# Two GroupNorm attention layers on one core: v twice-split from the third job, job 1's statistics by VectorE, and weight preparation spread over four attentions

## The chip, the cores and the metric

The kernel runs on one core of a Trainium2 chip. TensorE multiplies matrices, VectorE (DVE in the profile) and ScalarE (ACT) work on tensors element by element, GpSimd (POOL) here only starts transfers that add into memory, and SyncE (SP) starts the other transfers. Each engine takes its instructions in a fixed order. The metric is the device time of one execution in microseconds: 3188.19 us is the median of three runs of the kernel before (3187.46 to 3192.82).

## The reference

The input x is 8 images of 512 channels and 32 by 32 points, in fp32. Two layers follow one another, of one form with weights of their own. Cut to what is computed for one image:

```python
xg = x.reshape(8, -1)                                   # 8 groups of 64 channels
xn = (xg - mean(xg)) * rsqrt(var(xg) + 1e-5) * gamma + beta
q, k, v = Wq @ xn + bq, Wk @ xn + bk, Wv @ xn + bv      # 512 x 512 on 512 x 1024
for head in range(8):                                   # d = 64, s and t are points
    a = softmax(q_h.T @ k_h * 64 ** -0.5, axis=-1)      # 1024 x 1024
    out_h = v_h @ a.T
x = x + Wp @ out + bp
```

## The kernel before

**Jobs and stages.** One image in one layer is a job. Sixteen jobs run in the order images 0 and 1 in layer 0, the same images in layer 1, then images 2 and 3 in layer 0, and so on. So jobs 0 and 1 are layer 0, jobs 2 and 3 layer 1. Stages alternate. The attention A(n) of job n computes scores, exponentials and values. The projection stage P(n+1) then computes v of job n+1, the output projection of job n, and k and q of job n+1. P0 stands ahead of all, and a last output projection of job 15 at the end.

**Projections.** Products of 512 by 512 weights with 512 by 1024 activations use the Strassen-Winograd scheme, which makes seven block products out of eight, with sums of blocks made before (factors of the weights, sums of the activations) and after (VectorE additions of the products). The scheme is applied once (`v_phase`, L552: seven products of half size, 56 matmuls) or twice (`deep_phases`, L645: 49 products of quarter size). K, Q and the output (O) are twice-split in every stage but the very last; v is once-split for the jobs below `DEEP_V` and twice-split from it on. The lists `ORDER`, `OUTER`, `OUTER_V` say in which order the seven outer products go.

**Weight factors.** A twice-split product needs 49 factors of each weight. They are made once and kept in device memory, and each outer product's seven come in as one tile of 448 KB. They are made in two ways. `deep_round` (L212) takes a whole raw weight in, makes the outer factors by four additions (512 elements on each partition), the inner ones by four more (896), and stores seven tiles. A `prepare` (L199) instead makes the inner factors of one outer block when that block comes in for its first use, in a projection stage, by four short additions, and stores them. A once-split weight, or one to be prepared, needs its outer factors first: `put_first` loads raw weights, makes four additions for each (`factor`, L159) and stores them (`store_factors`, L170). `ROUNDS` and `FIRST` (L55, L56) say in which attention which weight and layer is done. Rounds, raw weights, the sums for twice-split projections (`deep_steps`, L1337) and `w_last` of the very last projection all take one buffer, the tag "deep", one after the other.

**Fetches.** A ring of up to six weight tiles is fetched ahead by `fetch` (L178) along `plan`. These tiles, the exponentials of the attention and parts of projection results share a pool of twelve buffers, given out in turn: a tile waits until the last readers of the tile that held its buffer are done.

**Attention.** 64 steps, in eight groups of eight (a group is two heads and half of the queries). A step computes scores of 128 keys by 1024 (L1112), their exponentials on ScalarE (L1117), and the values (L1163). VectorE sums the exponentials of a group into `acc` for the denominators (L1131, L1133). Of a group's eight tiles the first four are added as two pairs: GpSimd starts a transfer that adds one tile into another (L1140), and VectorE adds the result (L1143). At a group's end `take` brings the values out of PSUM (L1184 on ScalarE, L1186 on VectorE) and `reduce` sums `acc` over partitions (L1198). After each second group the denominators are gathered by small transfers (`r<-r`, L1221), inverted (L1225 on), written to memory (`rd<-rt`, L1238), broadcast back (`rb<-rd`, L1240), and multiplied in (L1255). The last pair does this without transfers, at the `times` set under `ends`.

**What sets the order.** The orders of TensorE, ScalarE and VectorE are the program's. `put` places a chore at an attention step and moves on to the next step where one is there; `moves` holds transfers by step; `later` and `advance` place small steps by a planned clock of 1.71 us a step. The orders of SP and GpSimd are made by the tile framework from the program and its plan of times. Norm steps: eight `stat` reads (L283), a gather by transfers, `groups`, `factors` (L355), four `apply` passes on ScalarE (L360), then four sums of xn (`sums`, L1305). For job 1 the statistics are instead eight ScalarE passes, `Norm.sums` (L293) and `Norm.squares` (L301). For jobs 2 to 4 the reads lie in the projection stages P1 to P3; from job 5 on in the attention before.

Of the kernel before, what the change touches and what calls it, by code (L numbers as in the profile page):

```python
# [19 lines left out]
P = 128  # L20
# [19 lines left out]
NW = 7  # L40
# [13 lines left out]
DEEP_V = 4  # L54
ROUNDS = {0: (O, 0), 2: (O, 1), 3: (V, 0), 4: (V, 1)}  # L55
FIRST = {0: ((V, 1),), 1: ((K, 1), (Q, 1))}  # L56
# [25 lines left out]
def fast_path(  # L82
# [129 lines left out]
    def deep_round(which, layer):  # L212
# [17 lines left out]
        def store_outer():  # L230
            w = box[0][:, :, 0:4, :].rearrange("p f (c h) o -> p f c (h o)", c=2)
            store_factors(w, layer, which)

# [10 lines left out]
        return start, first, store_outer, second, [lambda o=o: store(o) for o in OUTER]  # L244
# [159 lines left out]
    def norm_steps(n):  # L404
# [5 lines left out]
        def factors():  # L410
            norm.factors(slice(0, NC))
            if n > 1:
                place()

        if n == 1:
            reads = [place] + [lambda cc=cc: norm.sums(cc) for cc in range(NC)]
            reads.append(norm.less_mean)
            reads += [lambda cc=cc: norm.squares(cc) for cc in range(NC)]
            reads.append(lambda: (norm.by_count(), norm.gather()))
            return reads, [norm.groups, factors] + [lambda cc=cc: norm.apply(cc) for cc in range(NC)]  # L420
# [587 lines left out]
    def last_weights(n):  # L1008
        w = acts.tile([P, NW, 2, CH], F32, tag="deep", name="w_last")
        layer = jobs[n][1]  # L1010
        load_blocks(w, layer, O)
        for s in (slice(S1, NW), slice(S3, S3 + 1)):
            nc.sync.dma_start(w[:, s], factors[O, layer][:, s])
        return w
# [76 lines left out]
    class Attention:  # L1091
# [101 lines left out]
        def reduce(self, g):  # L1193
# [65 lines left out]
            if ends:  # L1259
                times = (0.0, 0.2, 7.6, 8.2) if n + 1 >= DEEP_V else (0.0, 0.2, 2.0, 4.0)  # L1260
            for at, step in zip(times, (gather, invert, spread, normalise)):
                later(at, step)
# [288 lines left out]
    for n in range(-1, len(jobs)):  # L1551
        last = n + 1 == len(jobs)
        outs = None
        if n >= 0:
# [7 lines left out]

            def put_round(which, layer):
                load, first, store_outer, second, stores = deep_round(which, layer)
                moves[9] = load
                at = 12
                for fn in first:
                    at = put(at + 1, fn)
                if (which, layer) == (O, 1):
                    moves[at + 1] = store_outer  # L1570
                    at += 4
                for fn in second:
                    at = put(at + 1, fn)
                at = max(at, 30 if n == 0 else 25)
                for i, fn in enumerate(stores):
                    at += 1 + i % 2
                    moves[at] = fn

            def put_first(weights):
                at = 43 if n == 0 else 5  # L1580
                box = []

                def start():
                    box.append(acts.tile([P, 2, NW, 2, CH], F32, tag="deep", name=f"raw_{n}"))
                    for i, (which, layer) in enumerate(weights):
                        load_blocks(box[0][:, i], layer, which)

                moves[at] = start
                at += 3
                for i, (which, layer) in enumerate(weights):  # L1590
                    for part in range(4):
                        at = put(at + 1, lambda i=i, part=part: factor(box[0][:, i], part))
                    moves[at + 1] = lambda i=i, which=which, layer=layer: store_factors(
                        box[0][:, i], layer, which
                    )

            if last:
                w = last_weights(n)
                for i, fn in enumerate(last_sums(0)):
                    put(49 + 3 * i, fn)  # L1600
            else:
                for i, (_, fn) in enumerate(extra):
                    put(2 + i, fn)
                at = (10, 19, 22, 24, 26, 28, 36, 39, 42, 45)
                if n == 0:
                    for i, fn in zip((3, 3, 4, 5, 6, 8, 10, 11, 12, 13, 15), reads):
                        put(i, fn)
                    at = (22, 30, 34, 35, 37, 38, 41, 44, 47, 50)
                elif n >= DEEP_V:
# [3 lines left out]
                elif n + 1 == DEEP_V:  # L1613
                    at = (10, 19, 22, 24, 26, 28, 30, 32, 35, 38)
                for i, fn in zip(at, steps):
                    put(i, fn)
                if n in ROUNDS:
                    put_round(*ROUNDS[n])
                if n in FIRST:
                    put_first(FIRST[n])  # L1620
# [4 lines left out]
                if n + 1 >= DEEP_V:  # L1625
                    for at, fn in zip((37, 39, 41, 43, 45, 47, 49, 51), deep_first):
                        put(at, fn)
                else:
                    for at, fn in zip((57, 58, 59, 60), deep_first[4:]):
                        put(at, fn)  # L1630

                def begin_plan():
                    extend_plan(n + 1)
                    if n + 1 < DEEP_V:
                        for _ in range(RING):
                            fetch()

                put(61 if n + 1 < DEEP_V else 58, begin_plan)
                if n + 1 >= DEEP_V:
                    for at in (58, 59, 60, 61, 62, 63):  # L1640
                        moves[at] = fetch
            assert max([*chores, *moves], default=0) < NT * len(att.groups)
# [27 lines left out]
            if last:  # L1670
                for i, fn in enumerate(last_sums(1)):
                    later(7.0 + 0.8 * i, fn)
# [13 lines left out]
            if n == 1:  # L1686
# [269 lines left out]
```

## Time and profile before

| What | us |
|---|---|
| Median of three runs | 3188.19 |
| The profiled execution | 3193.6 |
| Its span in the profile | 3191.7 |
| Matmul busy time | 3160.1 |
| VectorE busy time | 2612.1 |
| ScalarE busy time | 2312.2 |
| GpSimd busy time | 283.6 |

The profile is of one execution, so that each duration in the text is one of that execution. Matmuls are pipelined and their ends are modelled. A wait is put down to the releaser that came last. An attention followed by a projection stage takes 195.7 us from job 5 on. The last attention lies from 3048.0 to 3158.2 us of the span, and the last projection's matmuls end at 3184.2.

### The profile page before, as it was taken

How to read it: one execution, taken by the hardware profiler on the slowest of the kernel's cores; microseconds unless marked ns; L12 is line 12 of the kernel's file. 1: busy time of each engine (PE TensorE's matmuls, PEld its weight loads, DVE VectorE, ACT ScalarE, POOL GpSimd, SP SyncE). 2: the span in 40 equal slices, each digit the busy share in tenths (PEclk: the TensorE clock that was granted, in tenths of full speed). 3: DMA queues.
4: the chain of work that ended last, by engine and by line, in shares of the span. 5: the costliest groups of instructions: out<-in, count | busy, mean ns of one | idle time of the engine just before them, and what ended most of it. 6: DMA issues, size and time to landing. Idle time of an engine off the chain costs nothing.

```text
span 3191.7 us, 61670 instructions
## 1 busy us (share of the span) xinstructions
PE 3160.1 (99%) x23925; PEld 1872.0 (59%) x23925; DVE 2612.1 (82%) x3541; ACT 2312.2 (72%) x4169; POOL 283.6 (9%) x318
## 2 busy tenths in 40 slices
PE   9989999999999999999999999999999999999998
PEld 7356383573845738466393664837548375573844
DVE  8797787868979788797888969789697887978957
ACT  6747666486777868777686776867768687686863
POOL 0100101001000010100101000010000100001000
PEclk9999999999999999999999999999999999999999
DMA  7645565465655455355564545446456463444743
GB/s 276 151 133 151 121 200 142 120 188 135 204 158 145 120 110 172 74 145 164 139 190 83 158 103 138 125 94 177 132 137 182 90 199 66 135 122 95 221 91 77
DMA packets 189162, 451.70 MB, mean 142 GB/s; under 512 B 38088, under 2 KB 56896, under 8 KB 188864
## 3 DMA queue, kind: packets, MB, share of 16 engines
q1 hardware_dynamic: 140016, 298.27, 27.4%
q0 software_dynamic: 48848, 149.44, 25.8%
q8 instruction: 190, 3.11, 0.4%
q14 instruction: 108, 0.88, 0.1%
HBM read 246.76 MB, written 50.26 MB: 93 GB/s over the span
## 4 chain that ended last, share of the span: by engine, by line
PE 81%; DVE 3%; DMA 1%; issue 1%; ACT 0%; SPq 0%; DVEq 0%; ACTq 0%
PE sc L1112 23%; PE po L1163 22%; PE zd L817 9%; PE vd L817 9%; PE yd L817 4%; PE ud L817 4%; PE vd L812 3%; PE zd L812 3%; PE ud L812 1%; PE yd L812 1%; DVE acc L1133 1%; PE z L564 0%; DVE acc L1143 0%; PE z_last L1055 0%; DMA r<-r 0%
## 5 line engine op out<-in xcount | busy, mean ns | idle before, releaser
L1117 ACT ACTIVATE e<-sc 128x1024 f32<-128x1024 f32 x1024 | 1043.8, 1025 | 575.8 <-PE sc L1112 539.5
L1163 PE MATMUL po<-e,v 64*64 64x512 f32 x8192 | 1060.1, 590 | 9.8 <-ACT e L1117 9.8
L1112 PE MATMUL sc<-q,k 64*64 64x512 f32 x8192 | 1058.5, 590 | 2.2 <-ACT e L1117 2.0
L1163 PEld LDWEIGHTS po<-e,v 64*64 64x64 f32 x8192 | 313.3, 133 | 576.9 <-issue 540.2
L1112 PEld LDWEIGHTS sc<-q,k 64*64 64x64 f32 x8192 | 310.7, 133 | 566.7 <-issue 506.9
L1133 DVE TENSOR_TENSOR acc<-acc,e 128x1024 f32<-128x1024 f32 x320 | 389.4, 1217 | 42.2 <-ACT e L1117 31.9
L1140 POOL DMA_DIRECT2D e<-e x224 | 192.4, 859 | 1766.2 <-ACT e L1117 1279.8
L1143 DVE TENSOR_TENSOR acc<-acc,e 128x1024 f32<-128x1024 f32 x224 | 272.4, 1216 | 10.9 <-DMA e<-e 9.1
L1131 DVE TENSOR_TENSOR acc<-e,e 128x1024 f32<-128x1024 f32 x128 | 156.4, 1222 | 146.9 <-ACT e L1117 146.9
L817 PE MATMUL zd<-deep,w 128*128 128x256 f32 x860 | 240.2, 379 | 0.0
L817 PE MATMUL vd<-deep,w 128*128 128x256 f32 x804 | 223.5, 379 | 0.0
L817 PEld LDWEIGHTS zd<-deep,w 128*128 128x128 f32 x860 | 163.2, 190 | 22.5 <-ACT ud L512 0.3
L817 PEld LDWEIGHTS vd<-deep,w 128*128 128x128 f32 x804 | 152.7, 190 | 20.8
L1198 DVE TRANSPOSE_TENSOR_REDUCE r<-acc 128x32 f32<-128x1024 f32 x128 | 159.3, 1245 | 4.3
L912 POOL DMA_DIRECT2D x<-p x61 | 72.9, 1195 | 969.8 <-ACT p L834 427.1
L859 DVE TENSOR_TENSOR p<-p,s 128x512 f32<-128x512 f32 x185 | 127.2, 688 | 30.0 <-ACT p L834 22.3
L859 DVE TENSOR_TENSOR q<-q,s 128x512 f32<-128x512 f32 x64 | 44.1, 689 | 84.5 <-ACT q L836 44.1
L817 PE MATMUL vd<-os,w 128*128 128x256 f32 x372 | 107.2, 379 | 0.0
L812 PE MATMUL vd<-w,deep 128*128 128x128 f32 x720 | 102.2, 275 | 1.1 <-ACT ud L512 1.1
L817 PE MATMUL zd<-os,w 128*128 128x256 f32 x348 | 97.3, 379 | 1.3 <-ACT yd L508 1.3
L1186 DVE TENSOR_TENSOR q<-po,px 128x512 f32<-128x512 f32 x116 | 79.0, 681 | 22.7 <-ACT px L1184 22.5
L859 DVE TENSOR_TENSOR k<-k,s 128x512 f32<-128x512 f32 x64 | 44.2, 691 | 64.1 <-ACT k L834 42.8
(294 smaller groups left out, 4875.1 us busy)
## 6 DMA issues: line engine op xcount, KB each, us to landing
w<-deep SPq DMA_DIRECT2D x385, 448.0 KB, 5.1
e<-e POOLq DMA_DIRECT2D x224, 512.0 KB, 4.7
x<-p POOLq DMA_DIRECT2D x61, 512.0 KB, 6.8
rb<-rd SPq DMA_DIRECT2D x96, 256.0 KB, 3.7
x<-x_dram SPq DMA_DIRECT2D x28, 512.0 KB, 6.9
out_dram<-x SPq DMA_DIRECT2D x28, 512.0 KB, 4.1
deep<-w SPq DMA_DIRECT2D x28, 448.0 KB, 3.9
deep<-round SPq DMA_DIRECT2D x28, 448.0 KB, 4.7
```

The costliest lines, as they stand in the source:

```text
L812: nc.tensor.matmul(ps[:, tokens], moving[i][:, tokens], lhs[:, FACTOR[i], :], start=(start and ti == 0), stop=True, skip_group_check=True,)
L817: nc.tensor.matmul(ps, lhs[:, FACTOR[i], :], moving[i], start=start, stop=True, skip_group_check=True,)
L859: nc.vector.tensor_add(to_, to_, five.to_broadcast([P, 2, QT]))
L1112: nc.tensor.matmul(sc[h * HD : (h + 1) * HD, j, :], k[r, hp, k0 : k0 + HD], q[r, hp, sh * HALF : (sh + 1) * HALF], start=True, stop=True,)
L1117: nc.scalar.activation(e, sc, AF.Exp, scale=SCALE)
L1131: nc.vector.tensor_add(acc[g], self.es[i - 1], e)
L1133: nc.vector.tensor_add(acc[g], acc[g], e)
L1140: nc.gpsimd.dma_start(self.summed[i], self.summed.pop(i - 1), accum_op=ALU.add)
L1143: nc.vector.tensor_add(self.acc[g], self.acc[g], self.summed.pop(i))
L1163: nc.tensor.matmul(po[g][j * HD : (j + 1) * HD, h, :], v[r, kc, d0 : d0 + HD], e[r, j, :], start=(kc == 0), stop=(kc == NT - 1),)
L1186: nc.vector.tensor_add(to_, p[:, 1, :], px)
L1198: nc.vector.tensor_reduce(self.r[:, 0, m, :], self.acc.pop(g).rearrange("p j (b e) -> p (j b) e", e=RP), AX.X, ALU.add, apply_transpose=True,)
```

## The change

The change has six parts.

1. `DEEP_V` goes from 4 to 2: v of jobs 2 and 3 is twice-split. The conditions on `DEEP_V` move with it: from A1 on the attention is followed by the combined stage with v's sums made in the attention (`deep_steps`, all eight), and the last pair's `times` are the longer ones.
2. Rounds: O of layer 0 stays in A0, V of layer 1 moves from A4 to A1, O of layer 1 stays in A2, V of layer 0 stays in A3. The outer factors of layer 1's V are no longer made. K's of layer 1 are made in A0 and Q's in A1, where both were made in A1.
3. Job 1's statistics are made in A0 by `stat` on VectorE, at the steps at which the later attentions have theirs, and no longer by ScalarE. The reads for jobs 3 and 4 move from P2 and P3 into the attentions that follow these, A2 and A3; only those for job 2 stay in P1.
4. Placing: norm steps, round, deep sums and raw loads get other steps; the six fetches go one a step from 59 in every attention; transfers get a `move` that seeks the next free step, as `put` does.
5. The outer factors of layer 1's O are not stored. The last attention makes them from the raw blocks by four additions at steps 12, 14, 16 and 18. The last normalisation is at 7.0 on the planned clock (8.2 before), its transpose at 2.0 (7.6 before), and the last sums begin at 7.1 (7.0 before).
6. The second layer's output bias is made in P1 in place of P2.

```diff
-DEEP_V = 4
-ROUNDS = {0: (O, 0), 2: (O, 1), 3: (V, 0), 4: (V, 1)}
-FIRST = {0: ((V, 1),), 1: ((K, 1), (Q, 1))}
+DEEP_V = 2
+ROUNDS = {0: (O, 0), 1: (V, 1), 2: (O, 1), 3: (V, 0)}
+FIRST = {0: (K, 1), 1: (Q, 1)}
...
-        if n == 1:
-            reads = [place] + [lambda cc=cc: norm.sums(cc) for cc in range(NC)]
-            reads.append(norm.less_mean)
-            reads += [lambda cc=cc: norm.squares(cc) for cc in range(NC)]
-            reads.append(lambda: (norm.by_count(), norm.gather()))
-            return reads, [norm.groups, factors] + [lambda cc=cc: norm.apply(cc) for cc in range(NC)]
         reads = [lambda cc=cc, sh=sh: norm.stat(cc, sh) for cc in range(NC) for sh in range(2)]
...
         load_blocks(w, layer, O)
-        for s in (slice(S1, NW), slice(S3, S3 + 1)):
-            nc.sync.dma_start(w[:, s], factors[O, layer][:, s])
         return w
...
                 times = (0.0, 0.2, 7.6, 8.2) if n + 1 >= DEEP_V else (0.0, 0.2, 2.0, 4.0)
+                if n + 1 == len(jobs):
+                    times = (0.0, 0.2, 2.0, 7.0)
...
             def put_round(which, layer):
-                load, first, store_outer, second, stores = deep_round(which, layer)
-                moves[9] = load
-                at = 12
+                load, first, second, stores = deep_round(which, layer)
+                begin = {0: 6, 1: 12}.get(n, 9)
+                move(begin, load)
+                at = begin + 3
                 for fn in first:
                     at = put(at + 1, fn)
-                if (which, layer) == (O, 1):
-                    moves[at + 1] = store_outer
-                    at += 4
                 for fn in second:
                     at = put(at + 1, fn)
-                at = max(at, 30 if n == 0 else 25)
+                at = max(at + 3, 25)
                 for i, fn in enumerate(stores):
-                    at += 1 + i % 2
-                    moves[at] = fn
-
-            def put_first(weights):
-                at = 43 if n == 0 else 5
+                    at = move(at + 1 + i % 2, fn)
+
+            def put_first(which, layer):
+                at = move(37 if n == 0 else 3, lambda: start()) + 3
...
             if last:
                 w = last_weights(n)
+                for part in range(4):
+                    put(12 + 2 * part, lambda part=part: factor(w, part))
...
-                at = (10, 19, 22, 24, 26, 28, 36, 39, 42, 45)
-                if n == 0:
-                    for i, fn in zip((3, 3, 4, 5, 6, 8, 10, 11, 12, 13, 15), reads):
-                        put(i, fn)
-                    at = (22, 30, 34, 35, 37, 38, 41, 44, 47, 50)
-                elif n >= DEEP_V:
+                if n == 1:
+                    at = (8, 14, 15, 16, 18, 19, 21, 24, 27, 30)
+                else:
                     for i, fn in zip((3, 3, 4, 5, 5, 6, 7, 7, 8), reads):
                         put(i, fn)
                     at = (16, 22, 23, 24, 26, 27, 29, 31, 33, 35)
-                elif n + 1 == DEEP_V:
-                    at = (10, 19, 22, 24, 26, 28, 30, 32, 35, 38)
+                    if n < DEEP_V + 2:
+                        at = (17, 23, 24, 25, 27, 28, 30, 32, 34, 36)
...
                 if n + 1 >= DEEP_V:
-                    for at, fn in zip((37, 39, 41, 43, 45, 47, 49, 51), deep_first):
+                    for i, fn in enumerate(deep_first):
+                        put((42 if n in ROUNDS else 37) + 2 * i, fn)
+                else:
+                    for at, fn in zip((50, 52, 54, 56), deep_first[4:]):
                         put(at, fn)
-                else:
-                    for at, fn in zip((57, 58, 59, 60), deep_first[4:]):
-                        put(at, fn)
-
-                def begin_plan():
-                    extend_plan(n + 1)
-                    if n + 1 < DEEP_V:
-                        for _ in range(RING):
-                            fetch()
-
-                put(61 if n + 1 < DEEP_V else 58, begin_plan)
-                if n + 1 >= DEEP_V:
-                    for at in (58, 59, 60, 61, 62, 63):
-                        moves[at] = fetch
+                move(58, lambda: extend_plan(n + 1))
+                for _ in range(RING):
+                    move(58, fetch)
...
-            if n == 1:
+            if n == 0:
                 load, bias_steps = make_out_bias(1)
```

## The prediction

> **What bounds the kernel.** The busy shares first: TensorE is busy 99% of the span and the chain that ended last lies on it for 81%, so other engines matter only where TensorE waits for them.
>
> ```profile
> PE 3160.1 (99%) x23925; PEld 1872.0 (59%) x23925; DVE 2612.1 (82%) x3541; ACT 2312.2 (72%) x4169; POOL 283.6 (9%) x318
> PE 81%; DVE 3%; DMA 1%; issue 1%; ACT 0%; SPq 0%; DVEq 0%; ACTq 0%
> ```
>
> Then the stages, cut at the first matmul of each. Columns: start and end, length, busy time of PE, PEld, DVE, ACT, POOL, granted clock, DMA share, GB/s. The rows are A0, P1, A1, P2, A2, P3, A3, P4, A4, P5, A5 (A an attention, P a projection stage).
>
> ```profile
> 78.80:196.90 118.10, 111.69 (x1026) 39.15 (x1025) 90.82 (x115) 80.67 (x92) 12.93 (x15) 0.97 0.59 145
> 196.90:286.80 89.90, 88.05 (x410) 76.90 (x406) 72.26 (x109) 62.73 (x156) 4.79 (x4) 1.00 0.46 135
> 286.80:396.90 110.10, 110.10 (x1026) 39.32 (x1025) 86.50 (x104) 73.17 (x76) 13.23 (x15) 1.00 0.57 136
> 396.90:487.00 90.10, 88.31 (x411) 76.64 (x407) 79.49 (x161) 59.98 (x156) 4.77 (x4) 1.00 0.62 189
> 487.00:604.30 117.30, 111.81 (x1026) 38.55 (x1025) 91.73 (x115) 72.91 (x76) 17.26 (x15) 0.99 0.58 137
> 604.30:697.80 93.50, 90.88 (x410) 78.63 (x406) 69.92 (x104) 62.74 (x156) 5.99 (x5) 0.97 0.60 180
> 697.80:807.90 110.10, 110.10 (x1025) 39.06 (x1024) 93.30 (x113) 73.18 (x76) 12.61 (x15) 1.00 0.56 133
> 807.90:895.80 87.90, 86.25 (x491) 77.83 (x490) 71.54 (x102) 74.48 (x196) 4.77 (x4) 1.00 0.65 206
> 895.80:1006.60 110.80, 110.61 (x1026) 38.67 (x1025) 100.59 (x123) 73.14 (x76) 12.59 (x15) 1.00 0.59 149
> 1006.60:1092.10 85.50, 85.50 (x494) 77.61 (x490) 67.62 (x99) 75.45 (x196) 4.77 (x4) 1.00 0.47 140
> 1092.10:1202.20 110.10, 110.10 (x1026) 39.07 (x1025) 95.23 (x115) 73.05 (x76) 12.62 (x15) 1.00 0.50 115
> ```
>
> The last two rows are the steady pair, 110.1 + 85.5 (85.6 between first matmuls), and TensorE never pauses in it. A0 and A2 lose 8.1 and 7.3 us, A4 0.7; P1 to P4 are 4.3, 4.5, 7.9 and 2.3 longer than steady. Beyond A4 nothing can be gained. The waits that end in A0:
>
> ```profile
> ACT e L1117 <- DVE acc L1143: 8.5, 1, 8.5
> DVE lt L1225 <- DMA r<-r: 7.0, 1, 7.0
> PE po L1163 <- ACT e L1117: 6.4, 1, 6.4
> ```
>
> Read upwards from TensorE: it waited 6.4 us for one exponential, which waited 8.5 us for a VectorE addition. Step 61 fetches six weight tiles at once from the twelve buffers that exponentials share, so the next exponential needs the buffer of a recent pair, and VectorE was late, after 7.0 us behind a gather. A2 has the same wait (3.4), and P1 and P3 open with 1.9 us behind `DVE q L1186`: VectorE's last addition is done 6.57 and 6.33 us after A0 and A3, against 1.24 after A5.
>
> **What the Trainium skill says.** "Perfetto Trace Analysis", Optimization Strategy: kernels have several regimes, and within one the gaps of the contended engine are followed to what they wait for. The table agrees: 99% hides 28 us in nine stages. "TensorE: Matmul & The Clock Gate", Part 1: an idle window of about 3.4 us halves the clock until TensorE has been busy again. A0 agrees: a 6.4 us wait, 8.1 lost, clock 0.97. "DMA: Bandwidth & Descriptors", Issuing engines are not separate DMA queues: all issuers share sixteen engines. The trace agrees: accumulating pair DMAs of A0 land after 5.1 us in the middle, but after 8.4 and 11.2 beside seven stores of 448 KB. "VectorE: DVE Perf Modes", The TRN2 errata: an fp32 addition takes (N+151)/0.96 ns; 1224 for 1024, measured 1217.
>
> **1. v twice-split for jobs 2 and 3.** Once-split v is 56 matmuls of 0.43 us, 24 us; twice-split it is 49 products of two 128-wide halves, 0.446 a product, 21.9. P2 and P3 lose 2.1 each. Their VectorE work grows by the deep v's additions, 13.3 for 2.7; in P2 the eight reads of statistics (6.3) and the output bias (2.9) leave, but the preparations of K and Q stay (each four factors of 0.29 and a wait for the tile): 79.5 + 10.6 − 9.2 = 81 of VectorE where a steady stage has 67, so I add 0.7. P2 85.6 + 0.7 = **86.3**, P3 and P4 **85.6**: the stalls at their openings go, because a deep v needs its second PSUM half later. P4 also loses 2.3: its attention no longer ends late.
>
> **2. Fetches one a step instead of six at once (A0), last deep sums at 50 to 56.** The exponential before the end then needs an addition about six steps old. Both TensorE waits of A0 and A2 (6.4 and 3.4, with the slow clock 8.1 and about 5) go if VectorE is no more than some 6 us behind. The cover is that slack.
>
> **3. Job 1's statistics.** Eight ACT passes leave A0, 4.2 + 4.6 + 1.6 for reading accumulators = 10.4 us of ACT (80.7 to 70). In come eight statistics on VectorE and four aggregations, 8×0.68 + 4×0.21, = 6.3 at steps 3 to 8. The factors of V1 (4×0.68) give way to K1's, the same. VectorE in A0: 90.8, and 5.3 that fell past its end (6.57 late for 1.24), and 6.3: 102 of 110. Not a bound, but little slack. P1 takes the bias (four steps, 2.9), so it keeps its late opening: **91** for 90.0 (1.9 of stall become about 3).
>
> **4. The queue of SP in A0.** Here the order changes. In the kernel before the broadcast of the first normalisation is issued ahead of the seven stores of the round; the next raw load (same single buffer) comes after them:
>
> ```profile
> 121.40 0.33 SPq L1238 DMA_DIRECT2D rd<-rt  x1
> 121.78 1.14 SPq L345 DMA_DIRECT2D mr<-dg  x2
> 123.01 1.26 SPq L1240 DMA_DIRECT2D rb<-rd  x2
> 124.37 7.13 SPq L239 DMA_DIRECT2D deep<-round  x7
> 141.68 2.76 SPq L157 DMA_DIRECT2D raw<-wqkv_dram  x4
> ```
>
> The round now starts at step 6 and the load of K1 stands ahead of `rd<-rt` on SP. From first store to load were 17.3 us; seven stores (3.1 MB) now begin about 38 us into A0, the load issues near 51, `rd` 52, `rb` 54, and 256 KB land about **60** (56 to 64). VectorE, in order, reaches that normalisation at 48, so it idles some 12 us; behind it stand the accumulations that free exponentials' buffers. 102 + 12 is 4 past the end, and with the usual 1.2 to 4 behind the last exponential the last addition falls some 8 us after A0. That is about the slack of part 2: TensorE is stalled, one to one, only if `rb` lands later than 61. With 0.9 for an exponential behind a late application (part 5): A0 = **111.0**, bounds 110.1 and 116.
>
> **5. Rounds V1 in A1 and V0 in A3, O1 in A2, none in A4; norm steps moved.** A round costs VectorE 7.1. A1: 86.5 + 7.1 − 2.7 (K1's factors) + 4.5 (a deep v's first sums) + some 3 fallen past its end = 98. A2 and A3 now have what A4 had, 100.6, and A4 lost 0.7; A4 now has A5's 95. A4's loss is this wait:
>
> ```profile
> 936.62 1.24 ACT L360 ACTIVATE xn<-x,off,mul 128x1024 f32<-128x1024 f32 x1 [0.79 <-DVE off L355]
> ```
>
> It made the exponential behind it 1.9 late; in A5 1.1 is free. In A2 and A3 the factors stand at step 23 (22 in A4), and in VectorE's order the inversion (1.7) now precedes them: 2.85 late − 1.15 free = 1.7. A2 and A3 **111.8** each, bounds 110.1 and 113.5; A1 **110.2**, A4 **110.1**.
>
> **6. The last output's factors** are made by four additions of 0.68 at steps 12 to 18 of the last attention (VectorE 78 busy of 110), in place of two loads and of a store in A2: nothing, under that slack; uncovered 2.7. Its final transpose comes 5.6 us sooner (7.6 to 2.0), the normalisation 1.2 sooner; the last stage's wait is on a residual addition queued after it, so nothing, at best −0.5.
>
> **Sum.** A0+P1 202.0 for 208.2: −6.2. A1+P2 196.5 for 200.3: −3.8. A2+P3 197.4 for 211.0: −13.6. A3+P4 197.4 for 198.0: −0.6. A4 −0.7. Total **−24.9** on the profiled execution, 3193.6 (span 3191.7) to 3168.7. The median of the runs is 5.4 lower; I take the same difference from it: **3163**. If those 5.4 were stalls that the change removes, it would be 3169.
>
> **Rivals.**
> (a) Nothing stalls: A0 110.1, P1 90, P2 85.6, A2 and A3 110.1. Saves 31.5: **3157**. For it: steady stages never pause. Against: the queue of part 4.
> (b) VectorE stays the late engine: `rb` lands at 64 to 68 (another 3 to 5 in A0, with the slow clock), or A1 to A3 and P2, at 98 to 101 and 81, pass 2 to 4 us on. +6 to +8: **3170**. For it: A4 before lost time at this load. Against: fetches need no recent buffer.
> (c) The change doesn't do what it says: only the matmuls saved show (4.1) and the waits return at other steps: **3184**, no change by the 0.2% (6.4 us) that this kernel's measurement can tell.
> (d) Slower: the queue of part 4. Each us that `rb` lands past 61 costs TensorE one. At 86 it has eaten the 25 us, and beyond about 92 the kernel is slower than before by over 0.2%: **3195** or more. Stores of 3.1 MB would have to take over 40 us, where 17.3 were seen.
>
> **Chances.** Forecast 0.48, (a) 0.17, (b) 0.25, (c) 0.05, (d) 0.05. Range 3155 to 3175: from (a) less 2 to (b) plus 5. Faster 0.91 (forecast, a, b, a little off (c)), same 0.05, slower 0.04.
>
> **What would show it.** `DVE q L1242` waiting about 12 us on `rb<-rd` in A0 (part 4; if under 4, part 4 is wrong). A0 near 111, P1 91, P2 to P4 85.5 to 86.5; applications waiting on `off` in A2 and A3 (part 5; if these are 110.1, it was too dark). No `po` wait over 1 us at the ends of A0 and A2 (part 2). If P2 stays above 88, VectorE's preparations bound it; if a stage after A4 differs by over 0.3, an edit counted at nothing was not.

## The result, and the profile after

The changed kernel takes 3184.99 us (median of 20 runs, 3181.07 to 3187.94) where the kernel before takes 3189.54 (20 runs, 3184.10 to 3192.84): a ratio of 0.9986, with a 95% interval from 0.9979 to 0.9993. It is faster by 4.5 us, not by the 25 that were forecast, and lies outside the range of 3155 to 3175. Its profiled execution took 3187.94 us (span 3186.2), 5.7 less than that of before; it is the slowest of the 20.

The shares of busy time of the changed kernel, and its chain of work that ended last, hardly differ:

```profile
PE 3156.2 (99%) x24093; PEld 1872.4 (59%) x24093; DVE 2637.2 (83%) x3571; ACT 2333.5 (73%) x4233; POOL 281.0 (9%) x318
PE 81%; DVE 1%; issue 0%; DMA 0%; ACT 0%; SPq 0%; POOL 0%; DVEq 0%; ACTq 0%; POOLq 0%
```

The table by stage, with the columns of the prediction, for A0, P1, A1, P2, A2, P3, A3, P4, A4 of the changed kernel:

```profile
80.20:199.20 119.00, 112.04 (x1026) 37.78 (x1025) 93.44 (x123) 73.43 (x77) 13.84 (x15) 0.99 0.58 135
199.20:293.40 94.20, 91.44 (x407) 79.21 (x408) 77.56 (x121) 62.56 (x156) 4.79 (x4) 0.96 0.52 153
293.40:403.40 110.00, 110.00 (x1025) 39.02 (x1024) 93.80 (x112) 73.12 (x76) 12.59 (x15) 1.00 0.62 157
403.40:491.40 88.00, 86.05 (x494) 77.76 (x490) 81.54 (x157) 74.22 (x196) 4.77 (x4) 1.00 0.64 193
491.40:605.50 114.10, 110.52 (x1025) 38.86 (x1024) 101.13 (x123) 73.12 (x76) 13.45 (x15) 1.00 0.58 143
605.50:691.10 85.60, 85.60 (x498) 77.66 (x494) 67.61 (x99) 75.46 (x196) 5.99 (x5) 1.00 0.66 197
691.10:806.10 115.00, 111.81 (x1025) 37.72 (x1024) 99.80 (x122) 73.36 (x76) 13.46 (x15) 0.99 0.59 143
806.10:891.70 85.60, 85.60 (x498) 77.65 (x494) 68.72 (x100) 75.43 (x196) 4.77 (x4) 1.00 0.62 190
891.70:1001.70 110.00, 110.00 (x1026) 39.00 (x1025) 92.83 (x113) 73.10 (x76) 12.59 (x15) 1.00 0.48 105
```

| Stage (us between first matmuls) | before | forecast | after |
|---|---|---|---|
| A0 | 118.1 | 111.0 | 119.0 |
| P1 | 89.9 | 91 | 94.2 |
| A1 | 110.0 | 110.2 | 110.0 |
| P2 | 90.1 | 86.3 | 88.0 |
| A2 | 117.3 | 111.8 | 114.1 |
| P3 | 93.5 | 85.6 | 85.5 |
| A3 | 110.2 | 111.8 | 115.1 |
| P4 | 87.9 | 85.6 | 85.5 |
| A4 | 110.8 | 110.1 | 110.0 |

A steady attention takes 110.03 us and a steady projection stage 85.54, together 195.6. P3, P4 and A4 are steady as forecast, and so are all later stages and the end. Five stages are not: A0 is 8.0 over the forecast, P1 3.2, P2 1.7, A2 2.3, A3 3.3, together 18.5. P0, counted from its first matmul of `z` (L553), is 71.3 for 70.1, 1.2 over; with it and the few tenths that A1 and others are under, the 19.2 between the forecast of 3168.7 and the profiled execution is accounted for. In kernels made from the changed one P0 lies between 69.9 and 72.3, in the profile of before and those of two kernels made from it between 69.9 and 70.3; what makes some 1 us of that is left open.

The waits of A0, those of TensorE, VectorE and ScalarE:

```profile
PE sc L1099 <- ACT e L1104: 3.4, 1, 3.4
PE po L1150 <- ACT e L1104: 3.4, 1, 3.4
DVE q L1242 <- DMA rb<-rd: 17.6, 2, 14.7
DVE lt L1212 <- DMA r<-r: 3.1, 1, 3.1
ACT e L1104 <- DVE acc L1118: 5.4, 2, 4.6
ACT xn L356 <- DVE off L351: 4.4, 1, 4.4
```

TensorE stands twice for an exponential: once in the middle, when ScalarE waits 4.4 us for the norm's factors, and once at the end, when that exponential has waited 4.6 us for an addition of VectorE, which is late after 14.7 us behind a broadcast. A2 and A3 have the first kind only. In A2's order of time, VectorE then ScalarE:

```profile
533.74 0.59 DVE L1212 TENSOR_REDUCE lt<-r 32x64 f32<-32x256 f32 x1 [1.75 <-DMA r<-r]
...
536.91 0.16 DVE L351 TENSOR_TENSOR off<-vec_sb,off 128x4 f32<-128x4 f32 x1
537.11 1.24 ACT L356 ACTIVATE xn<-x,off,mul 128x1024 f32<-128x1024 f32 x1 [4.00 <-DVE off L351]
```

The factors stand behind the inversion in VectorE's order, and the inversion waits for its gather. SP's order of time in A0:

```profile
118.58 7.85 SPq L235 DMA_DIRECT2D deep<-round  x7
131.17 0.38 SPq L157 DMA_DIRECT2D raw<-wqkv_dram  x1
131.61 0.46 SPq L1225 DMA_DIRECT2D rd<-rt  x1
132.11 1.45 SPq L157 DMA_DIRECT2D raw<-wqkv_dram  x3
134.16 2.26 SPq L1227 DMA_DIRECT2D rb<-rd  x2
```

It is the order that the prediction named: the first store, the raw load, `rd` and `rb` are issued 38.4, 51.0, 51.4 and 54.0 us after A0's start. The landing of `rb` is read from the end of VectorE's wait, at 66.5.

### The profile page after: what moved, and what is told of

It reads as the page before. It is cut to its first block, busy times and chain, and to the rows that moved or that the text cites. A ratio compares the mean times of both kernels' runs of the same rounds, so it can differ in the third digit from the quotient of the medians.

```text
span 3186.2 us, 62139 instructions
## 1 busy us (share of the span) xinstructions
PE 3156.2 (99%) x24093; PEld 1872.4 (59%) x24093; DVE 2637.2 (83%) x3571; ACT 2333.5 (73%) x4233; POOL 281.0 (9%) x318
## 4 chain that ended last, share of the span: by engine, by line
PE 81%; DVE 1%; issue 0%; DMA 0%; ACT 0%; SPq 0%; POOL 0%; DVEq 0%; ACTq 0%; POOLq 0%
PE sc L1099 23%; PE po L1150 23%; PE zd L806 9%; PE vd L806 9%; PE yd L806 4%; PE ud L806 4%; PE vd L801 4%; PE zd L801 3%; PE yd L801 1%; PE ud L801 1%; DVE acc L1120 0%; PE z_last L1042 0%; DMA r<-r 0%; ACT e L1104 0%; DVE x L1064 0%
## 5 line engine op out<-in xcount | busy, mean ns | idle before, releaser
L801 PE MATMUL vd<-w,deep 128*128 128x128 f32 x840 | 119.1, 275 | 1.1 <-ACT ud L501 1.1
L801 PE MATMUL zd<-w,deep 128*128 128x128 f32 x728 | 106.5, 275 | 0.9 <-ACT ud L501 0.9
L801 PEld LDWEIGHTS vd<-w,deep 128*128 128x128 f32 x840 | 106.2, 192 | 1.3 <-ACT ud L501 1.3
```

What stands on the lines that cost most here:

```text
L801: nc.tensor.matmul(ps[:, tokens], moving[i][:, tokens], lhs[:, FACTOR[i], :], start=(start and ti == 0), stop=True, skip_group_check=True,)
```

## The experiments

The theory at first: A0's first stall and those of A2 and A3 come from the place of the norm's factors (part 5 of the prediction), A0's second stall and P1's from SP's queue (part 4). The rival: VectorE has too much to do in these attentions, so that its waits only move. Kernels with one execution are read by their stages. A stage in which TensorE never waits repeats closely: A1 is 110.03 or 110.04 us in all 16 profiles. A stage with waits need not: A0 is 119.0 us in the changed kernel and 116.5 in a kernel whose one edit lies in A1, and P1 is 88.8 and 89.9 in two executions of one kernel. So in such stages a difference of up to some 2.5 us shows little by itself, and the waits are read with it.

**Factors at step 22 in A0, A2 and A3.**

```diff
-                    if n < DEEP_V + 2:
-                        at = (17, 23, 24, 25, 27, 28, 30, 32, 34, 36)
```

> The changed kernel, but the norm steps of A0, A2 and A3 take the steps of the later attentions (factors at 22, not 23), which puts the factors on VectorE ahead of the inversion, and of its wait for the gather. Theory (ScalarE's application waits 4.0 to 4.4 us for off, because off stands behind an inversion that waits for a gather): the wait falls to about 1, A2 goes from 114.1 and A3 from 115.1 to 110.0 to 110.8 each, A0 from 119.0 to 114.5; 12 us in all. Rival (VectorE is the bound in A2 and A3 with 101 us): they stay above 112, or P3 and P4 open with 2 us of waits instead of 85.5.

The rows of this kernel for A0, P1, A2 and A3:

```profile
81.50:195.60 114.10, 110.94 (x1025) 38.58 (x1025) 93.77 (x123) 73.40 (x77) 12.93 (x15) 1.00 0.59 142
195.60:289.50 93.90, 91.38 (x409) 79.26 (x409) 77.26 (x121) 62.26 (x156) 4.79 (x4) 0.96 0.52 152
486.80:597.60 110.80, 110.61 (x1026) 38.61 (x1025) 101.12 (x123) 73.14 (x76) 12.61 (x15) 1.00 0.59 147
683.10:793.90 110.80, 110.61 (x1026) 38.69 (x1025) 99.50 (x122) 73.14 (x76) 12.61 (x15) 1.00 0.60 146
```

A2 and A3 are 110.8 with VectorE as busy as before (101.1 and 99.5), and their P3 and P4 stay at 85.5: VectorE is no bound there. ScalarE's wait for `off` falls from 4.4 us to 0.5 in A0 and from 4.0 to 0.8 in A2. A0 is 4.8 shorter than the changed kernel's. The three together are 12.5 us, in a time of 3175.45: one step in the order of VectorE. P1 keeps 93.9, and VectorE still waits 14.3 us for the broadcast.

**The round of A0 at step 12, alone.**

```diff
-                begin = {0: 6, 1: 12}.get(n, 9)
+                begin = {0: 12, 1: 12}.get(n, 9)
```

> The changed kernel, but the round of A0 begins at step 12 instead of 6, so that SP issues the broadcast of the first normalisation ahead of the seven stores and of K1's raw load. Theory (the broadcast behind the raw load costs A0 its second stall of 3.4 us and some 1 us of slow clock, and P1 its 2.8 us wait and slow clock): the 14.7 us wait of VectorE on rb<-rd falls under 3, A0 goes from 119.0 to 114 to 115 (its first stall, behind the late off, stays), P1 from 94.2 to 90 to 91; 8 us in all. Rival (VectorE has too much work in A0, 102 us and more, so that its waits only move): A0 stays at 117 to 119 and P1 above 93.

A0 118.5, P1 94.6: nothing gained, as the rival said. VectorE's waits in A0:

```profile
DVE lt L1212 <- DMA r<-r: 9.5, 2, 7.8
...
DVE q L1242 <- DMA rb<-rd: 3.3, 1, 3.3
```

The broadcast is early now, but the second gather stands behind the same raw load, which waits for later stores. SP's order of time:

```profile
151.53 3.42 SPq L157 DMA_DIRECT2D raw<-wqkv_dram  x4
155.00 1.84 SPq L1208 DMA_DIRECT2D r<-r  x3
```

This run alone can't tell a moved queue from too much work.

**Without K1 in A0** (with factors at step 22).

```diff
                 if n == 0:
-                    put_first(*FIRST[n])
+                    factors[K, 1] = factors[Q, 0]
```

> The kernel with factors at step 22, and without the raw load, the four additions (2.7 us of VectorE) and the store of K1 in A0; layer 1's K takes its outer factors from another weight's store instead, so that part of the computation is left out. The broadcast follows the seven stores at once. Theory (what is left in A0, 4.1 us, and P1's 6 us over a quiet stage come from transfers of the attention queued behind the raw load, which waits for the stores): rb<-rd lands near 53 us after A0's start, VectorE waits under 6 for it instead of 14.3, A0 is 110 to 111, P1 90 to 91.5. Rival (VectorE's work after the middle of A0 is more than the time left, and its waits only move, as when the round was begun later): A0 stays at 113 or more and P1 above 93.

A0 is 111.2 and P1 91.7; VectorE waits 9.1 us for the broadcast, not under 6. Most of A0's loss is gone with the raw load, though the 2.7 us of additions left out may count too.

**K1's raw load by GpSimd** (with factors at step 22; the round at step 6, then at step 12).

```diff
-                nc.sync.dma_start(w[:, 2 * j + i], raw_block(layer, which, i, j))
+                queue.dma_start(w[:, 2 * j + i], raw_block(layer, which, i, j))
...
-                    load_blocks(box[0], layer, which)
+                    load_blocks(box[0], layer, which, nc.sync if n else nc.gpsimd)
```

> The kernel with factors at step 22 and K1's raw load issued by GpSimd instead of SP, the round of A0 at step 6 as in the changed kernel. It is the same computation as the changed kernel. Theory: the broadcast follows the stores directly and VectorE's 14.3 us wait falls to 5 to 7; A0 110 to 111.5, P1 90 to 91.5, A2 and A3 110.8, P2 87.3; in all 20 us below the changed kernel, some 3165. Rival: GpSimd, waiting for the stores with the raw load, holds up the pairs behind it and VectorE waits for e<-e instead; A0 stays at 113 or more, and the whole near 3172.

3168.86 us, a ratio to before of 0.9935 (0.9918 to 0.9952). A0 111.3, P1 92.0, VectorE's wait 8.6: A0 as expected, the wait longer than 5 to 7, and P1 and the time above what was expected.

> The kernel with factors at step 22, the round of A0 begun at step 12, and K1's raw load issued by GpSimd instead of SP, so that neither the first broadcast nor the second gather stands behind it. Theory: the waits of VectorE on r<-r and rb<-rd in A0, 7.8 and 3.3 when only the round was begun later, fall to under 5 together; A0 110 to 111.5, P1 90 to 92. Rival (the work itself): A0 above 113, P1 above 93.

A0 110.4, P1 88.8, a time of 3164.07. All work of A0 is there, additions too, so the rival falls: VectorE had the time, it spent it waiting. In exchange VectorE waits 4.9 us in all for pairs, which GpSimd holds back behind the raw load. The same kernel timed:

> The kernel of the second GpSimd run (factors at step 22, the round of A0 at step 12, K1's raw load by GpSimd), timed. Its single look had a span of 3162.3. Theory: 3162 to 3167, 0.7% to 0.8% below the kernel before, and below the changed kernel's 3185 by 18 to 23. Rival (the look was a lucky one of a kernel like the one with the round at step 6): 3168 to 3170.

3166.07 us (3164.67 to 3168.79), 0.9930 (0.9916 to 0.9943). The profile of these five runs has A0 at 110.4 and P1 at 89.9.

**The two edits of place alone: factors at step 22 and the round at step 9 or 12, K1 by SP.** In the kernels so far, the place of the transfers had been changed together with the queue of the raw load.

```diff
-                begin = {0: 6, 1: 12}.get(n, 9)
+                begin = {0: 9, 1: 12}.get(n, 9)
...
-                    if n < DEEP_V + 2:
-                        at = (17, 23, 24, 25, 27, 28, 30, 32, 34, 36)
```

> The changed kernel with factors at step 22 and the round of A0 begun at step 9, where the kernel before had it; K1's raw load stays with SP, after the broadcast and ahead of the second gather. Theory (with the statistics early, the place of the first broadcast among the stores decides A0; a second gather behind the raw load costs VectorE about 3 us, which it can make up): VectorE waits under 5 for the first broadcast, A0 110 to 111.5, P1 88 to 90, A2 and A3 110.8; 3164 to 3168 in all, about the kernel with GpSimd. Rival (the raw load on SP is what costs, wherever it stands): A0 113 or more.

3165.29 us (3164.87 to 3165.80), 0.9919 (0.9902 to 0.9935): this beats the kernel before and the changed kernel, and is not told apart from the one with GpSimd by the intervals; no engine was given other work. A0 and P1, and SP's order in A0:

```profile
80.40:191.50 111.10, 110.78 (x1026) 38.64 (x1025) 99.86 (x128) 73.14 (x76) 12.93 (x15) 1.00 0.63 156
191.50:279.30 87.80, 87.80 (x410) 76.98 (x406) 71.59 (x116) 62.73 (x156) 4.79 (x4) 1.00 0.52 150
```

```profile
119.90 2.01 SPq L235 DMA_DIRECT2D deep<-round  x3
122.93 0.37 SPq L1225 DMA_DIRECT2D rd<-rt  x1
123.35 1.37 SPq L235 DMA_DIRECT2D deep<-round  x2
127.23 1.31 SPq L1227 DMA_DIRECT2D rb<-rd  x2
128.58 1.07 SPq L235 DMA_DIRECT2D deep<-round  x2
136.83 2.02 SPq L157 DMA_DIRECT2D raw<-wqkv_dram  x4
144.76 1.84 SPq L1208 DMA_DIRECT2D r<-r  x3
```

The broadcast is issued between stores, 7 us before where it was, and the raw load is over before the second gather is due. VectorE waits 3.0 us for the broadcast in place of 14.7, 0.7 for the second gather, and no longer for the first, which had cost it 3.1.

> The same with the round begun at step 12: broadcast ahead of all stores, stores later, so the raw load and the second gather behind it are later too. Theory (the latest of the attention's transfers in SP's queue decides): the second gather stands behind a raw load that waits for later stores, VectorE waits some 7 us for it as with factors at 23, and A0+P1 is 3 to 6 us more than with the round at step 9. Rival (only the first broadcast counts): the same as with step 9.

A0 113.6, P1 91.4, with 7.6 us of VectorE for the second gather and 3.5 for its broadcast: 6.1 us more than at step 9 for the two stages together. So both places count, and at step 9 neither is in the way.

**Fetches one a step, in the kernel before** (part 2 alone).

```diff
-                put(61 if n + 1 < DEEP_V else 58, begin_plan)
-                if n + 1 >= DEEP_V:
-                    for at in (58, 59, 60, 61, 62, 63):
-                        moves[at] = fetch
+                moves[57] = lambda: extend_plan(n + 1)
+                for at in (58, 59, 60, 61, 62, 63):
+                    moves[at] = fetch
```

> The kernel before with one edit: the six fetches of A0, A1 and A2 go one a step from step 58, not all at step 61. Theory (part 2 of the prediction: the stalls at the ends of A0 and A2, 6.4 and 3.4 us with the slow clock after them, come from six buffers taken at once): A0 goes from 118.1 to 110 to 111.5, A2 from 117.3 to 112 to 113 (its stalls of 2.0 behind late applications stay). Rival (VectorE's lag of 6.6 us stalls the exponentials anyway): A0 stays at 115 or more. P1 keeps its 1.9 us wait in both.

TensorE's waits in A0 and P1:

```profile
PE sc L1112 <- ACT e L1117: 4.2, 1, 4.2
PE v L564 <- DVE q L1186: 4.1, 1, 4.1
```

A0 goes to 116.8 and A2 to 115.3 only, and what is gained is lost at once: A0 and P1 together are 211.5 for 208.1, A2 and P3 210.3 for 210.8. The kernel takes 3196.35 us, more than any run of the kernel before. Not even A2's 2.0 can be put down to the fetches: A2 is 115.5 in the kernel with the statistics alone, below, whose fetches of A0 to A2 stay at step 61. VectorE's lag was the cause, as that kernel shows, whose A0 doesn't stall; the buffers only chose where the lag showed.

**The fetches back at step 61**, in the kernel timed above with GpSimd:

```diff
-                for _ in range(RING):
-                    move(58, fetch)
+                if n == 0:
+                    move(61, lambda: [fetch() for _ in range(RING)])
+                else:
+                    for _ in range(RING):
+                        move(58, fetch)
```

> The same timed kernel, but the six fetches of A0 all at step 61, as before the change. Theory (fetches one a step give slack of some four more steps: with VectorE 6 us late at A0's end, the exponentials of the last steps need a recent pair's buffer again): A0 goes from 110.4 to 112 to 116, P1 stays near 89. Rival (spreading the fetches is worth nothing once VectorE is in time, as it was worth nothing in the kernel before): A0 stays under 111.

A0 111.2 for 110.4, between what theory and rival expected: with VectorE in time, the fetches are worth 0.8 us in A0 (110.4 in all three executions that have them one a step).

**Statistics by VectorE, in the kernel before** (part 3 alone, with the norm steps of the later attentions).

```diff
-        if n == 1:
-            reads = [place] + [lambda cc=cc: norm.sums(cc) for cc in range(NC)]
...
-                if n == 0:
-                    for i, fn in zip((3, 3, 4, 5, 6, 8, 10, 11, 12, 13, 15), reads):
-                        put(i, fn)
-                    at = (22, 30, 34, 35, 37, 38, 41, 44, 47, 50)
-                elif n >= DEEP_V:
+                if n == 0 or n >= DEEP_V:
```

> The kernel before with part 3 alone: job 1's statistics by VectorE at steps 3 to 8 of A0, and the norm steps of the later attentions (groups at 16, factors at 22, sums to 35). Theory (A0's losses are transfers of the attention queued behind the stores and the next raw load, whatever VectorE has to do): the second gather stays behind the raw load of V1, VectorE waits some 7 us for it and 3 to 5 for a broadcast; A0 and P1 together stay within 3 us of the 208.1 of the kernel before. Rival 1 (6.3 us more on VectorE overload it): A0 and P1 together 4 us longer or more. Rival 2 (statistics off ScalarE and sums placed earlier are a gain of their own): 4 us shorter or more.

A0 and P1 of this kernel:

```profile
80.00:190.80 110.80, 110.61 (x1025) 38.78 (x1024) 97.89 (x127) 73.14 (x76) 12.94 (x15) 1.00 0.63 156
190.80:278.70 87.90, 87.90 (x414) 77.02 (x410) 70.27 (x107) 62.73 (x156) 4.79 (x4) 1.00 0.48 135
```

198.7 for 208.1: 9.4 us gained, and my theory of the moment missed it. The six fetches at step 61 and a raw load ahead of the second gather are still there. VectorE has 6.3 us more to do and stands idle in waits over 0.3 us for 10.8 instead of 25.9. The profile of before has among them 6.1 us for late exponentials early in A0, while ScalarE made statistics, 4.1 for pairs and 7.0 for the gather:

```profile
DVE acc L1131 <- ACT e L1117: 6.1, 2, 4.1
DVE acc L1143 <- DMA e<-e: 4.1, 2, 3.4
```

With the statistics by VectorE the pairs cost no wait over 0.3 us, and the other two are:

```profile
DVE lt L1218 <- DMA r<-r: 2.9, 1, 2.9
DVE acc L1124 <- ACT e L1110: 2.2, 2, 1.9
```

But the run moves two things, the engine of the statistics and the steps of the norm and its sums, which are earlier, and with them the transfers: the round's stores begin 39.3 us into A0 in place of 45.6, and the raw load is issued at 56.4 in place of 62.9. How much of the 9.4 each of these brings isn't shown.

**Statistics back to ScalarE**, at their old steps, in the kernel with GpSimd:

```diff
...
+        if n == 1:
+            reads = [place] + [lambda cc=cc: norm.sums(cc) for cc in range(NC)]
...
+                if n == 0:
+                    for i, fn in zip((3, 3, 4, 5, 6, 8, 10, 11, 12, 13, 15), reads):
+                        put(i, fn)
+                    at = (22, 30, 34, 35, 37, 38, 41, 44, 47, 50)
```

> The same timed kernel, but job 1's statistics by eight ScalarE passes at their old steps, with the old steps of the norm (groups at 22, factors at 30, sums at 41 to 50). VectorE has 6.3 us less to do in A0, and four sums of 1.14 come later. Theory (only the work after VectorE's last idle time counts): the 6.3 us were done in time that is idle anyway, the late sums lengthen the lag, A0+P1 goes from 199.2 to 202 to 206. Rival (the sum of the work counts, 102 of 110): A0+P1 falls, or stays within 1 us.

A0 and P1 are 207.8 for 200.4, more than expected, but not for the reason given. GpSimd's order of time in A0:

```profile
127.35 0.89 POOL L1134 DMA_DIRECT2D e<-e  x1 [5.76 <-ACT e L1111]
141.84 2.91 POOL L157 DMA_DIRECT2D raw<-wqkv_dram  x4 [13.61 <-DMA deep<-round]
144.73 2.75 POOL L1134 DMA_DIRECT2D e<-e  x3
```

Three pairs stand behind the raw load, which waits for the stores; VectorE waits 12.1 us for the first of them. It is the same mechanism on another queue, so the run says nothing on the statistics themselves.

**P2, and VectorE's lag at the end of A1.** In the changed kernel VectorE's last addition of exponentials of A1 ends 6.4 us after the first matmul of P2. This is called its lag here. (The prediction's 6.57 and 6.33 for A0 and A3 of before are the same lags, counted from rounded times; they are 6.64 and 6.26.) Two runs tried to shorten it, the first in the changed kernel.

```diff
-                at = begin + 3
+                at = begin + (5 if n == 1 else 3)
```

> The changed kernel, but the round's additions of A1 are placed two steps later (its load stays at 12), so that VectorE does attention work while the round's load lands. Theory (the 2.5 us that P2 loses are the lag of VectorE at the end of A1, 6.4 us, and this lag is the sum of its waits early in A1: 3.1 for the round's load, 2.2, 1.6, 1.0): the 3.1 wait goes, the lag falls to about 3.5, P2 goes from 88.0 to 85.6 to 86.3. Rival (P2 loses by its four preparations of K and Q, with VectorE at 81.5 busy): P2 stays at 88.

The 3.1 us wait fell to 0.5, other waits (1.6 and 2.8) came, the lag is 5.5 and P2 87.1, short of the 86.3 that was expected. Even this gain isn't shown to be the edit's: in the nine other kernels here that have A1 as in the changed kernel, the lag is 5.2 to 5.8 and P2 86.9 to 87.9.

The second starts from the kernel with GpSimd and the round of A0 at step 12, which is the "same kernel" of its expectation.

```diff
-                begin = {0: 12, 1: 12}.get(n, 9)
+                begin = {0: 12, 1: 8}.get(n, 9)
...
-                    put_first(*FIRST[n])
+                    factors[Q, 1] = factors[Q, 0]
```

> The same kernel, but with the raw load, four additions and store of Q1 left out of A1 (layer 1's Q takes another weight's outer factors, so that part of the computation is left out), and the round of A1 begun at step 8, since its buffer is free sooner. Theory (P2's loss is VectorE's lag at the end of A1, and the lag is what work is left after VectorE last stood idle for an exponential, about 37 us into A1, because idle time before that can't be used): with the round's additions in that early idle time the lag falls from 5.3 to under 3.5, and P2 from 86.9 to 85.5 to 85.8. Rival (P2 is slow by its preparations of K and Q): P2 stays at 86.8 to 87.3.

The lag is 4.9 for 5.25 and P2 86.55 for 86.86: a miss of the expected 3.5 and 85.8. How to shorten the lag stays open. What it costs doesn't. Over the runs, lag and length (us) go together:

| Kernel, stage | lag of VectorE's last addition | length of the stage |
|---|---|---|
| without Q1, P2 | 4.94 | 86.55 |
| GpSimd, round at 12, P2 | 5.25 | 86.86 |
| factors at 22, P2 | 5.70 | 87.30 |
| changed kernel, P2 | 6.42 | 88.02 |
| before, P4 | 6.26 | 87.86 |
| place edits, round at 9, P1 | 3.01 | 87.82 |
| statistics alone, P1 | 4.46 | 87.83 |
| without Q1, P1 | 5.48 | 88.78 |
| before, P1 | 6.64 | 89.94 |
| without K1, P1 | 6.74 | 91.73 |
| changed kernel, P1 | 9.22 | 94.20 |

With a twice-split v the stage takes 85.54 us plus what the lag exceeds 3.94 by, to 0.01 us in the five rows. In all 16 profiles 30 twice-split stages have a lag over 3.94; 27 lie on this line, and three are 0.2 to 0.5 us above it. P4 of before, without any preparation, lies on the same line as P2, so in these P2 the preparations cost nothing that shows. With a once-split v the stage takes 87.82 plus the excess over 4.52, and 1.7 more in the last two rows, where the granted clock was 0.98 and 0.96. Of the 22 once-split stages in the profiles, nine lie on that line and 13 are 1.3 to 2.8 above it. P2 of before, which prepares too, is one of these: 90.1 at a lag of 5.3, with a TensorE wait of 1.3 us elsewhere in the stage (`zd` behind a copy of ScalarE) that the lag doesn't explain.

## Why the prediction was wrong

Two steps failed. Part 5 left the wait for the gather out of what the late factors cost, and part 4 had the landing of the broadcast and its price in P1 too small. Of the 19.2 us between forecast and profiled execution, an estimate from the stages and from the run with factors at 22 gives part 5 some 9.5 (2.3 in A2, 3.3 in A3, and 3.9 in A0, where 4.8 was lost for the 0.9 set) and part 4 some 7.3 (the other 4.1 of A0, and 3.2 in P1). P2 makes 1.7 and P0 1.2, less some tenths elsewhere. As A0 differs by 2.4 us between two executions, the split of its 8.0 is rough. The sum also had a slip: for before it took 208.2, 200.3 and 211.0, where its own table gives 208.0, 200.2 and 210.8, so that 0.5 us too much was saved.

**Part 1 held.** P3 and P4 are 85.5, a once-split stage without stalls 87.8, so the twice-split v saves 2.3 a job, where 2.1 was worked out. P2 is not quiet, though: the forecast took the opening stall away because "a deep v needs its second PSUM half later". It is later, but only by so much that a lag up to 3.9 is free.

**Part 2 had the wrong cause.** "Both TensorE waits of A0 and A2 go if VectorE is no more than some 6 us behind" was right only in its condition. The fetches are worth 0.8 us with VectorE in time and nothing without. That A0 can lose its stalls was right; what takes them away in the kernel before is part 3 with the norm's earlier steps, which the sum counted as a small burden.

**Part 3 was counted with the wrong sign.** The sum over the attention, "102 of 110", took work as cost and idle time as slack. In the kernel before, the statistics and the norm steps that go with them gain 9.4 us in A0 and P1, though VectorE has more to do; which of the two brings it stays open. ScalarE's work in A0 fell by 7.2 us (80.7 to 73.4), not by the 10.4 of the forecast, and nothing that was seen hung on it.

**Part 4, SP's queue, was the right mechanism with terms mis-sized.** The issue times are those of the forecast to 1 us. The landing is not: two transfers of 256 KB were given some 6 us after issue, and took 12.5 from the first issue to the end of VectorE's wait, beside 1 MB of raw blocks and two pairs. `rb` landed at 66.5, not 60, beyond the 64 of its upper bound. With factors at 22, where nothing delays A0 ahead of it, it landed at 62.7, and A0 was 4.1 over steady, of which A2 and A3 of that kernel have 0.7 too: so the point from which it decides is, by estimate, 62.7 − 3.4 = 59.3, where the forecast had 61. Landings at 57.5 and 58.1, with K1 by GpSimd and without K1, left A0 at 111.3 and 111.2. P1 was given 1 us for the later opening; it paid 4.7 over a quiet once-split stage for the lag of 9.2, and 1.7 where the clock fell.

**Part 5 left out a wait.** "The inversion (1.7) now precedes them: 2.85 late" counts the inversion's work and not the gather that it waits for (1.75 in A2, 1.9 in A3, 3.1 in A0). With the 1.75 the 2.85 becomes 4.6 in A2. ScalarE stood 4.0 to 4.4 us. TensorE waited 3.6 in A2 and 3.2 in A3, with a clock of 0.99 in A3, and the stages lost 4.0 and 5.0 over steady and, by the run with factors at 22, 4.8 in A0, where 1.7, 1.7 and 0.9 were set. At step 22 the loss is 0.7 in A2 and A3, as A4 of before showed.

**P2.** A1 was summed to 98 of 110 and P2 given 0.7. VectorE idles 14 us in A1, most of it in the first 38 us, and ends 6.4 late: 2.5 us, by the line above. The forecast's own sign, P2 above 88 for a bound by the preparations, was met at 88.02, but P4 of before, which prepares nothing, pays the same for its lag.

**Of the rivals**, the outcome is nearest to (c), by its number, but not by its mechanism: the waits did not return at other steps, two new ones took the place of the old. (b), at 0.25, had the landing of `rb` right (64 to 68) and about what it costs A0, and some microseconds in A2, A3 and P2, but as alternatives, for 6 to 8 us in all, and for A2 and A3 by VectorE's load, which wasn't the reason. Both came, and P1 with them. (d) named the right queue at a far larger size. The forecast's own bounds for `rb` and for the late application were both too narrow on the same side. With both waits taken away the kernel is 3165.29, 2 us from the forecast, but by another sum, so that this nearness is in part luck. P1 is 3.2 under the forecast, A2 and A3 1.0 each, P2 1.0 over.

## What to carry to other kernels

An instruction that is moved behind another in an engine's order inherits that one's waits, not only its time; so look for the last transfer that anything ahead of it needs. A transfer that waits for a buffer held back what was queued behind it on both queues tried here (14.7 us of VectorE on SP's, 12.1 on GpSimd's): place such loads where nothing urgent follows within the time that the buffer takes. And judge an engine that feeds another not by its sum but by how late it ends: here each us of lag past a free 4 to 4.5 costs one us, while 6.3 us more work, put where it had stood idle early in A0, did not make A0 longer.

## What the runs showed of the hardware that was not expected

TensorE's clock fell after a shorter pause than I had reckoned with. In the kernel without K1 and in the one timed with GpSimd, P1 opens with a wait of nearly the same length. TensorE's order of time, first without K1, then with GpSimd:

```profile
198.46 3.25 PE L553 MATMUL v<-w,t 128*128 128x256 f32 x8 [1.95 <-DVE q L1173]
```

```profile
197.89 1.99 PE L553 MATMUL v<-w,t 128*128 128x256 f32 x8 [1.83 <-DVE q L1173]
```

After 1.95 us the next eight matmuls take 3.25 us, after 1.83 us 1.99, and without K1 P1 is 1.7 us longer than its lag alone makes it. The Trainium skill, "TensorE: Matmul & The Clock Gate", Part 1, tells of an idle window of about 3.4 us; here a pause of little over half of it was enough, and the measurement decides. The length alone doesn't decide. In the kernel before, two waits of the same length open P3 and P1, and only the first is followed by slow matmuls:

```profile
612.45 3.41 PE L564 MATMUL v<-w,t 128*128 128x256 f32 x8 [1.86 <-DVE q L1186]
```

```profile
204.18 1.99 PE L564 MATMUL v<-w,t 128*128 128x256 f32 x8 [1.85 <-DVE q L1186]
```

What else decides isn't shown.

The broadcast of `rb<-rd`, 3.7 us from issue to landing in the median of the kernel, took 12.5 beside the raw load and two pairs. In the two runs with the same order of transfers (factors at 22; A1's additions later) it was issued 3 us later, 57.0 and 57.1 us into A0, and took 5.7 and 7.3. So its own size didn't set this time. That the transfers in flight beside it did is likely; no run isolates it.
